# A state-space mixer on one core: the opening of the kernel rearranged, and the later images' statistics in column tiles

## The chip, the cores and the metric

The kernel runs on one NeuronCore of a Trainium2 chip. A NeuronCore has five engines, each with its own queue of instructions that it works off in order: TensorE (PE in the profile; PEld is its loading of weights), VectorE (DVE), ScalarE (ACT), GpSimd (POOL) and SyncE (SP), which here only issues DMAs. They work at the same time and wait for each other through semaphores. Sixteen DMA engines move data between HBM (the large memory) and SBUF (the working memory of 128 partitions); matrix products land in PSUM, eight banks of 512 float32 numbers per partition. The metric is the device time of one execution in microseconds (us).

## The reference

Four images of 128 channels and 96 x 96 pixels are normalised per group of four channels, and each is read as a sequence in four directions (rows, columns, and both reversed). Each sequence goes through the same mixer, and the four results are fused and added to the input:

```python
def _scan1d(x, ...):
    t = _grouped1x1(x, in_proj_w, in_proj_b, G)
    u, gate = (t[:, :HID], t[:, HID:])
    u = jax.nn.silu(u)
    u = lax.conv_general_dilated(u, dw_w, ..., feature_group_count=HID)   # 5 taps
    s = _conv1x1(u, ssm_in_w)
    a = DMIN + (DMAX - DMIN) * jax.nn.sigmoid(_conv1x1(u, ssm_delta_w, ssm_delta_b))
    bb = jnp.tanh(_conv1x1(u, ssm_b_w, ssm_b_b))
    cc = jnp.tanh(_conv1x1(u, ssm_c_w, ssm_c_b))
    prefix = jnp.cumsum(jnp.log(a), axis=-1)
    hst = jnp.exp(prefix) * jnp.cumsum(bb * s * jnp.exp(-prefix), axis=-1)
    u = u + _conv1x1(cc * hst + ssm_d[None, :, None] * s, ssm_out_w)
    u = _grouped1x1(u * jax.nn.sigmoid(gate), mix_w, mix_b, G)
    return _conv1x1(u, out_proj_w, out_proj_b)
...
x = x + conv_ref(_gn(x), ...)      # four directions, then fuse_w, fuse_b
```

All numbers are float32.

## The kernel before

**Units of work.** A sequence is cut into `NS` = 6 stages of 16 lines; every fourth column belongs to one residue p, so a stage has R = 4 residues of N = 384 positions. A *pair* is one residue of one stage in a direction and its reverse: two units. An image has 24 pairs in the order V (columns), then 24 in H (rows): 192 pairs in all. `pair(t)` issues the work of pair t together with that of neighbours: the front of the stage R pairs ahead, the recurrence of earlier pairs, and the output (gate, mixing, accumulation in `acc`) of pair t - LAG = t - 6. The order on each engine is the order in which the program issues it; it is fixed by hand. `start()` issues what stands before pair 0, `tail()` what stands after the last.

**A front.** `in_proj` multiplies the rows `x_in` of a stage with the normalised weights `wn`, in 32x32 tiles of the array, four columns at a time; `silu` (L495 in ACT) takes it out of PSUM to `sil`, with the bias `bnorm`. A burst is the eight tiles of one half j and one residue g. Then `conv` and `conv_less` (PE, from `sil` with the weights `band` and `less`) give half of `u`, which ACT copies out (L632, L634), and `taps` gives the other half: tap 0 on ACT (L649), taps 1 to 4 on VectorE (L651), each waiting for the one before. `proj` multiplies u with `main` and ACT takes tanh of it (`tm`, L683), and with that the pair's recurrence can begin. The fronts of the later half of a sequence use `sil` kept in HBM by `keep_silu` and loaded back.

**Statistics.** `bn_stats` (L282 for image 0, from `acc`, into which x is loaded anyway; L412 for the later images, from chunks `xs` loaded one pair ahead in two buffers) takes 24 pieces of 384 columns per image. `stats_finish` is a generator whose pieces are issued between other work: bn_aggr, the group means by a product with `gmean` (L187), the variance (L199), the inverse deviation, the weights `wn` times it, and the biases by `wn` times the group means (L235 and sixteen 32x32 products in L238), read by VectorE (L239).

**The opening.** SP issues the loads of x (`load_x`, growing pieces) and then step 0's `x_in`; ACT's queue issues the loads of the weights `small`, `fuse` and `main`. At most eight DMAs are under way by the program's eight DMA semaphores: each issue waits for the eighth before it. POOL builds gmean, the identity, band and less. PE and ACT fold the output's weights: `w_of` = out_proj x fuse per direction (L364), `w_fin` = mix x w_of (L371), `b_fin` the bias (L379), before image 0's statistics are through; `stay_busy` (L286) are matmuls without use, 512 or 256 columns wide, put into the gaps. Then `start()`:

```python
        for g in range(R):
            burst(0, g)
        for g in range(R):
            silus(0, g)
        new_u(0)
        for g in range(R):
            burst(1, g)
            silus(1, g)
            after_front(0, g)
            ...
```

`after_front` issues on SP the loads of step 1's rows, one residue of half 1 at a time and half 0 after the last. `proj` of pair 0 has step 1's first front (residue 0) between its two halves.

Of the kernel before, what the change touches and what calls it, by code (L numbers as in the profile page):

```python
# [42 lines left out]
F32 = mybir.dt.float32  # L43
# [4 lines left out]
P = 128  # L48
# [8 lines left out]
R = 4  # L57
# [10 lines left out]
def conv_preact_kernel(  # L68
# [106 lines left out]

    def stats_finish(b):
# [10 lines left out]
        nc.tensor.matmul(pm[:, 0:1], gmean, mv[:, 0:1], start=True, stop=True)  # L187
# [10 lines left out]
        for e in range(2):  # L198
            nc.tensor.matmul(pv[:, e : e + 1], gmeans[:, e, :], ex, start=True, stop=True)  # L199
# [35 lines left out]
        nc.tensor.matmul(pb[:, 0:4], wn, gm4, start=True, stop=True)  # L235
        for g in range(4):
            for q in range(R):
                mm(pb[:, 4 + g : 5 + g], q, wn[0:32, 32 * g : 32 * g + 32], mean[0:32, :], True, True)  # L238
        nc.vector.tensor_sub(bn, b_in, pb[:, 0:8])  # L239
# [33 lines left out]
    def load(src, name, pool=wp):  # L273
        t = pool.tile(list(src.shape), F32, tag=name, name=name)
        nc.scalar.dma_start(t, src)
        return t
# [7 lines left out]
    def stay_busy(n):  # L284
        if n:
            nc.tensor.matmul(  # L286
                bank(free[0] ^ 1)[:, :n], w_fin[:, 0, 0, :],
                w_fin.rearrange("p d j c -> p (d j c)")[:, :n], start=True, stop=True,
                skip_group_check=True,
            )  # L290

# [6 lines left out]
    prep = tc.tile_pool(name="prep", bufs=1)  # L298
    pp = prep.__enter__()
    load_x([(0, 1), (1, 2), (3, 3)])  # L300
    w_small = load(small, "small")
    load_x([(6, 4)])
    w_out_fuse = load(fuse, "fuse", pp)
    load_x([(10, 4)])
    w_main = load(main, "main")
    load_x([(14, 4), (18, 4), (22, 2)])
    for s in range(2):
        load_front(0, s, half(s), slice(0, R))
    for i in range(UB):
# [13 lines left out]
    nc.vector.tensor_scalar_mul(b_proj[64:P, 0:1], b_proj[64:P, 0:1], 0.5)  # L323
    nc.vector.tensor_scalar_mul(
        w_proj[:, :, 2 * MH : 3 * MH], w_proj[:, :, 2 * MH : 3 * MH], 0.5
    )


# [11 lines left out]
    id32 = pp.tile([P, 32], F32, name="id32")  # L340
    ident = pp.tile([P, P], F32, name="ident")
# [18 lines left out]
    w_of = pp.tile([P, 4, 2, P], F32, name="w_of")  # L360
    for d in range(4):
        for j in range(2):
            pt = bank(2 * (d % 4) + j)
            nc.tensor.matmul(  # L364
                pt[:, :P], w_out[:, bass.ts(j, P)], w_fuse[:, d, :], start=True, stop=True
            )
            nc.scalar.copy(w_of[:, d, j, :], pt[:, :P])
    for d in range(4):
        for j in range(2):
            pt = bank(2 * (d % 4) + j)  # L370
            nc.tensor.matmul(  # L371
                pt[:, :P], w_mix[:, j, :], w_of[:, d, j, :], start=True, stop=True
            )
            nc.scalar.mul(w_fin[:, d, j, :], pt[:, :P], 0.5)
    pb = bank(0)
    terms = [(w_of[:, d, j, :], b_mix[:, j : j + 1]) for d in range(4) for j in range(2)]
    terms += [(w_fuse[:, d, :], b_out) for d in range(4)]
    for i, (lhsT, rhs) in enumerate(terms):
        nc.tensor.matmul(  # L379
            pb[:, 0:1], lhsT, rhs, start=(i == 0), stop=(i == len(terms) - 1)  # L380
        )
    nc.scalar.activation(b_fin, pb[:, 0:1], AF.Identity, bias=b_fuse)
    for _ in range(4):
        stay_busy(512)
    prep.__exit__(None, None, None)
# [19 lines left out]
    def load_chunks(t):  # L405
        for b, c in chunks_of(t):
            chunks[b, c] = wk.tile([P, SC], F32, tag="xs", name=f"xs_{b}_{c}")
            nc.sync.dma_start(chunks[b, c], xr[b, :, bass.ts(c, SC)])
# [721 lines left out]
```

## Time and profile before

| | us |
|---|---|
| runs shown | 1824.41, 1825.7, 1827.61 (median 1825.7) |
| the profiled execution | 1830.29 |
| its span, first to last instruction | 1828.6 |
| mean granted clock of TensorE | 0.993 of full |

The page gives busy time, its share of the span, and the number of instructions for each engine; then 40 equal slices of the span, a digit for tenths of a slice that an engine was busy:

```profile
PE   7999999999999999999999999999999999999998
ACT  4888888988888888898888888888888888888974
PEclk7999999999999999999999999999999999999999
```

Only the first slice (45.7 us) and the last are not full. PEclk is the clock granted to TensorE, in tenths. The waits of the first 55 us, by the waiting engine and line, who released it, and the sum, the number and the longest:

```profile
PE psum L364 <- DMA fuse<-in_fuse: 6.5, 1, 6.5
DVE bn L282 <- DMA acc<-in_xr: 3.3, 2, 1.7
PE psum L134 <- DMA x_in<-in_xs: 3.2, 1, 3.2
ACT psum L649 <- DVE u L651: 2.4, 1, 2.4
PE psum L187 <- DVE mv L184: 2.1, 1, 2.1
```

`mm`, the helper of all tiled products, is line 134, so groups of tiled matmuls are told apart by what they read and write: `psum<-x_in,wn` is in_proj, `psum<-sil,band` conv, `psum<-u,main` proj, `psum<-u,w_fin` the output.

### The profile page before, as it was taken

The page shows a single profiled execution, that of the slowest core. Times are in us where ns is not written, and L with a number is a line of the kernel's source. Part 1 is how long each engine was busy: PE and PEld are TensorE (multiplying, and loading weights), DVE is VectorE, ACT ScalarE, POOL GpSimd, SP SyncE. Part 2 cuts the span into 40 slices and gives each one's busy share as a digit, 9 for nine tenths or more (in the row PEclk, how much of TensorE's full clock was granted, in tenths as well). Part 3 has the DMA queues.
Part 4 walks back from the last instruction along what each step waited for, and adds up shares of the span by engine and source line. Part 5 has one row for each costly group of instructions (what it writes and reads, how often), then busy time and mean ns, then how long its engine had stood idle before and what let it go on. Part 6 is the DMA issues. An engine that isn't in the chain of part 4 may idle for free.

```text
span 1828.6 us, 56926 instructions
## 1 busy us (share of the span) xinstructions
PE 1805.3 (99%) x24068; PEld 653.1 (36%) x24068; DVE 1451.0 (79%) x1451; ACT 1566.5 (86%) x2762; POOL 1423.7 (78%) x1469
## 2 busy tenths in 40 slices
PE   7999999999999999999999999999999999999998
PEld 3333333333333333333333333333333333333333
DVE  5788878877788888887788888877877878777886
ACT  4888888988888888898888888888888888888974
POOL 2478887878778888777877888788778788887785
PEclk7999999999999999999999999999999999999999
DMA  5765464543975567244596557543477734535434
GB/s 182 205 199 173 148 189 116 169 156 130 278 260 180 167 180 214 98 147 139 180 306 224 167 169 207 141 142 120 159 230 221 245 126 152 192 106 179 148 122 156
DMA packets 147823, 321.17 MB, mean 176 GB/s; under 512 B 14192, under 2 KB 115696, under 8 KB 147568
## 3 DMA queue, kind: packets, MB, share of 16 engines
q1 hardware_dynamic: 147136, 316.56, 53.8%
q8 instruction: 190, 3.11, 0.7%
q10 hardware_dynamic: 432, 0.96, 0.1%
q14 instruction: 65, 0.53, 0.1%
HBM read 185.21 MB, written 132.25 MB: 174 GB/s over the span
## 4 chain that ended last, share of the span: by engine, by line
PE 96%; ACT 1%; DVE 1%; DMA 1%; issue 0%; SPq 0%; DVEq 0%
PE psum L134 83%; PE psum L520 8%; PE psum L514 5%; DMA acc<-in_xr 0%; DVE bn L282 0%; ACT sil L495 0%; DVE u L600 0%; ACT psum L649 0%; DMA x_in<-in_xs 0%; DVE psum L651 0%; PE psum L286 0%; ACT psum L528 0%; PE psum L199 0%; ACT u L632 0%; ACT t L689 0%
## 5 line engine op out<-in xcount | busy, mean ns | idle before, releaser
L651 DVE SCALAR_TENSOR_TENSOR psum<-sil,small,psum 128x768 f32<-128x768 f32 x576 | 589.1, 1023 | 35.1 <-ACT psum L649 8.3
L134 PE MATMUL psum<-u,w_fin 128*32 128x384 f32 x6176 | 552.3, 487 | 0.2 <-ACT t L689 0.2
L600 DVE SCALAR_TENSOR_TENSOR u<-gate,psum 128x768 f32<-128x768 f32 x376 | 349.8, 953 | 248.4 <-ACT gate L537 110.5
L134 PE MATMUL psum<-u,main 128*32 128x384 f32 x6144 | 536.4, 490 | 0.2
L770 POOL TENSOR_TENSOR acc<-ys,acc 128x384 f32<-128x384 f32 x374 | 410.7, 1119 | 31.2 <-ACT ys L751 9.2
L724 POOL TENSOR_TENSOR t<-t,t 64x384 f32<-64x384 f32 x191 | 232.2, 1216 | 154.6 <-DVE t L718 70.8
L134 PEld LDWEIGHTS psum<-u,w_fin 128*32 128x32 f32 x6176 | 188.8, 110 | 321.7 <-issue 216.5
L134 PEld LDWEIGHTS psum<-u,main 128*32 128x32 f32 x6144 | 182.0, 110 | 328.1 <-issue 198.9
L691 POOL TENSOR_SCALAR t<-tm 64x384 f32<-64x384 f32 x191 | 177.1, 927 | 153.7 <-ACT tm L683 100.1
L528 ACT COPY psum<-u 128x768 f32<-128x768 f32 x352 | 276.7, 799 | 22.0 <-DVE u L651 11.3
L134 PE MATMUL psum<-sil,band 128*32 128x384 f32 x3072 | 287.2, 491 | 0.0
L725 POOL TENSOR_TENSOR t<-t,t 64x384 f32<-64x384 f32 x191 | 246.5, 1291 | 15.0
L520 PE MATMUL psum<-t,main 32*128 32x384 f32 x1536 | 241.4, 513 | 3.3 <-ACT psum L528 2.6
L649 ACT ACTIVATE psum<-sil,small 128x768 f32<-128x768 f32 x192 | 174.1, 907 | 65.4 <-DVE u L600 54.9
L537 ACT ACTIVATE gate<-psum,bnorm 128x384 f32<-128x384 f32 x384 | 192.0, 582 | 30.2 <-PE psum L514 28.6
L692 POOL TENSOR_TENSOR t<-t,tm 64x384 f32<-64x384 f32 x192 | 195.1, 1016 | 15.4 <-ACT t L684 0.2
L651 DVE SCALAR_TENSOR_TENSOR u<-sil,small,psum 128x768 f32<-128x768 f32 x192 | 194.9, 1015 | 7.8
L495 ACT ACTIVATE sil<-psum,bnorm 128x385 f32<-128x385 f32 x384 | 192.3, 583 | 6.4 <-PE psum L134 4.3
L134 PE MATMUL psum<-sil,less 64*32 64x384 f32 x3072 | 168.1, 495 | 0.0
L514 PE MATMUL psum<-x_in,wn 32*128 32x384 f32 x768 | 157.5, 527 | 1.5 <-DVE bnorm L239 1.1
L727 POOL COPY t<-t 64x384 f32<-64x384 f32 x188 | 141.0, 750 | 15.5 <-PE psum L134 3.6
L134 PEld LDWEIGHTS psum<-sil,band 128*32 128x32 f32 x3072 | 90.8, 109 | 171.8 <-issue 95.5
(92 smaller groups left out, 1496.7 us busy)
## 6 DMA issues: line engine op xcount, KB each, us to landing
sil<-sil SPq DMA_DIRECT2D x128, 770.0 KB, 6.6
kept<-gate SPq DMA_DIRECT2D x80, 768.0 KB, 3.7
gate<-kept SPq DMA_DIRECT2D x76, 768.0 KB, 5.1
x_in<-in_xs SPq DMA_DIRECT2D x192, 96.2 KB, 2.5
out<-acc SPq DMA_DIRECT2D x48, 384.0 KB, 8.3
acc<-in_xr SPq DMA_DIRECT2D x38, 384.0 KB, 7.1
xs<-in_xr SPq DMA_DIRECT2D x72, 192.0 KB, 4.9
x_in<-in_xs SPq DMA_DIRECT2D x184, 48.1 KB, 4.0
```

Source lines behind the costliest of these rows:

```text
L134: nc.tensor.matmul(o[r, : rhs.shape[-1]], lhsT, rhs, start=start, stop=stop, skip_group_check=True)
L495: nc.scalar.activation(sils[step][:, s, j, g, :], bank(bk)[:, : N + 1], AF.Silu, bias=bn[:, 1:2] if j else bn[:, 4 + g : 5 + g],)
L514: nc.tensor.matmul(bank(to)[:, :N], stats[un["b"]][0][r, s, :], x_in[s][r, q, off : off + N], start=True, stop=True)
L520: nc.tensor.matmul(bank(SSM + 2 * s + j)[:, :N], w_so[r, bass.ts(j, P)], z[r, :], start=bi not in seeded, stop=True, skip_group_check=True)
L528: nc.scalar.copy(psum[:, SSM + 2 * s : SSM + 2 * s + 2, :N], us[bi][:, s])
L537: nc.scalar.activation(gv[:, s, j, :], bank(to[2 * s + j])[:, :N], AF.Tanh, bias=bn[:, 2 + j : 3 + j], scale=0.5,)
L600: nc.vector.scalar_tensor_tensor(v, g, 1.0, pz, ALU.add, ALU.mult)
L651: nc.vector.scalar_tensor_tensor(us[i][:, :, 1, :] if k == K - 1 else part, src, w_tap[:, k : k + 1], part, ALU.mult, ALU.add,)
L692: nc.gpsimd.tensor_mul(ta[0:64, p, :], tb[0:64, :], tm[0:64, :])
L724: engine.tensor_mul(ta[0:64, p, :], tb[64:P, :], ta[64:P, p, :])
L725: engine.tensor_add(tb[0:64, :], ta[0:64, p, :], tb[0:64, :])
L770: adder.tensor_add(part, y, part)
```

## The change

1. `load_x` takes x first and in smaller first pieces, all on SP; `fuse` and `main` come behind x on SP, and only `small` is issued by ACT. The scalings of `b_proj` and `w_proj` go from VectorE to POOL, behind band and less.
2. The folding of the output's weights moves into `start()`: `outer` (L364 before) between the pieces of the statistics, with one copy per direction on ACT (three) or VectorE (one); `inner` between the bursts, taken out by VectorE two directions at a time. `b_fin` is summed over directions by POOL (four additions) and then needs three matmuls instead of twelve, behind pair 0's conv. `filler`, matmuls on loaded x, replaces `stay_busy`: five of 512 columns and one of 128.
3. `start()` is in a new order, given below; pair 0's first tap is on VectorE; the loads of step 1's rows (`load_rows`) and the keeping of step 0's sil stand in `start()`. In pair 0's `proj` the front of step 1 stands before both halves, with the next pair's first tap in its middle.
4. The chunks `xs` of the later images are loaded two pairs ahead, in four buffers.
5. The products of the statistics are column tiles (`product`: four of 32 columns). For the later images the biases of the 32x32 kind come from one small copy, one product with the mask and four tiles with the identity, one piece later than before. Where a pair accumulates two waiting units, a piece of the statistics stands ahead of conv_less.

```diff
 
+    def product(o, lhsT, rhs):
+        for c in range(4):
+            mm(o, c, lhsT[:, 32 * c : 32 * c + 32], rhs, True, True)
+
...
-        nc.tensor.matmul(pm[:, 0:1], gmean, mv[:, 0:1], start=True, stop=True)
+        product(pm[:, 0:1], gmean, mv[:, 0:1])
...
-        nc.tensor.matmul(pb[:, 0:4], wn, gm4, start=True, stop=True)
-        for g in range(4):
+        product(pb[:, 0:4], wn, gm4)
+        if b == b0:
+            for g in range(4):
+                for q in range(R):
+                    mm(pb[:, 4 + g : 5 + g], q, wn[0:32, 32 * g : 32 * g + 32], mean[0:32, :], True, True)
+            nc.vector.tensor_sub(bn, b_in, pb[:, 0:8])
+        else:
+            nc.vector.tensor_sub(bn[:, 0:4], b_in[:, 0:4], pb[:, 0:4])
+            spread = sp.tile([P, 4], F32, tag="spread", name=f"spread_{b}")
+            shift = sp.tile([P, 1], F32, tag="shift", name=f"shift_{b}")
+            nc.vector.tensor_copy(shift, pb[:, 0:1])
+            nc.vector.tensor_scalar_mul(spread, gmask, shift)
+            yield
+            pq = bank(free[0])
             for q in range(R):
-                mm(pb[:, 4 + g : 5 + g], q, wn[0:32, 32 * g : 32 * g + 32], mean[0:32, :], True, True)
-        nc.vector.tensor_sub(bn, b_in, pb[:, 0:8])
+                mm(pq[:, 0:4], q, id32, spread, True, True)
+            nc.vector.tensor_sub(bn[:, 4:8], b_in[:, 4:8], pq[:, 0:4])
...
-    load_x([(0, 1), (1, 2), (3, 3)])
-    w_small = load(small, "small")
-    load_x([(6, 4)])
-    w_out_fuse = load(fuse, "fuse", pp)
-    load_x([(10, 4)])
+    w_small = load(small, "small", nc.scalar)
+    load_x([(0, 1), (1, 1), (2, 1), (3, 2), (5, 2), (7, 3), (10, 4), (14, 4), (18, 4), (22, 2)])
+    w_out_fuse = load(fuse, "fuse")
     w_main = load(main, "main")
-    load_x([(14, 4), (18, 4), (22, 2)])
...
+    nc.gpsimd.tensor_scalar_mul(b_proj[64:P, 0:1], b_proj[64:P, 0:1], 0.5)
+    nc.gpsimd.tensor_scalar_mul(
+        w_proj[:, :, 2 * MH : 3 * MH], w_proj[:, :, 2 * MH : 3 * MH], 0.5
+    )
...
-            chunks[b, c] = wk.tile([P, SC], F32, tag="xs", name=f"xs_{b}_{c}")
+            chunks[b, c] = wk.tile([P, SC], F32, tag="xs", bufs=4, name=f"xs_{b}_{c}")
...
-            if k == 0:
+            if k == 0 and first:
+                first.tensor_scalar_mul(part, src, w_tap[:, 0:1])
+            elif k == 0:
                 nc.scalar.activation(part, src, AF.Copy, scale=w_tap[:, 0:1])
...
-            if i == 0 and (e, j) == (0, 1):
-                front(R, (5, 4, 2, 3))
+            if i == 0 and (e, j) == (0, 0):
+                first = front_parts(R, (5, 4, 2, 3), half=True)
+                next(first)
+                next(first)
+                first_tap(2)
+                for _ in first:
+                    pass
...
             accumulate(waiting.pop(0), w[1], *final)()
             free[0] = w[0]
+            stats_piece()
             if not between:
                 conv_less(i, banks)
-            stats_piece()
         if old:
...
-        if t + 1 < NU // 2:
-            load_chunks(t + 1)
+        if t + 2 < NU // 2:
+            load_chunks(t + 2)
...
-        keep_silu((1, 2, 1, 0)[t] if t < R else 0)
...
+        w_of = wp.tile([P, 4, 2, P], F32, name="w_of")
+        def filler(n):
+            nc.tensor.matmul(
+                bank(7)[:, :n], accf[:, bass.ds(10 * SC, P)], accf[:, bass.ds(10 * SC, n)],
+                start=True, stop=True,
+            )
+        def outer(d, i, copy):
+            for j in range(2):
+                nc.tensor.matmul(
+                    bank(i)[:, bass.ts(j, P)], w_out[:, bass.ts(j, P)], w_fuse[:, d, :],
+                    start=True, stop=True,
+                )
+            copy(w_of[:, d].rearrange("p j c -> p (j c)"), bank(i)[:, : 2 * P])
+        def inner(ds, i):
+            for n, (d, j) in enumerate((d, j) for d in ds for j in range(2)):
+                nc.tensor.matmul(
+                    bank(i)[:, bass.ts(n, P)], w_mix[:, j, :], w_of[:, d, j, :],
+                    start=True, stop=True,
+                )
+            to = w_fin[:, ds[0] : ds[-1] + 1].rearrange("p d j c -> p (d j c)")
+            nc.vector.tensor_scalar_mul(to, bank(i), 0.5)
         pieces = stats_finish(b0)
-        for wait in (0, 256, 512, 0, 0):
-            next(pieces, None)
-            stay_busy(wait)
+        for n in (512, 512, 512):
+            filler(n)
+        next(pieces)
+        for n in (512, 512):
+            filler(n)
+        next(pieces)
+        outer(0, 0, nc.scalar.copy)
+        outer(1, 1, nc.scalar.copy)
+        next(pieces)
+        outer(2, 4, nc.scalar.copy)
+        next(pieces)
+        outer(3, 5, nc.vector.tensor_copy)
+        filler(128)
+        for _ in pieces:
+            pass
         sils[0] = wk.tile([P, 2, 2, 4, N + 1], F32, tag="sil", name="sil_0")
-        banks = ((2, 3), (4, 5), (6, 7), (0, 1)), ((2, 3), (4, 5), (2, 3), (4, 5))
+        banks = ((2, 3), (6, 7), (0, 1), (4, 5)), ((2, 3), (6, 7), (4, 5), (2, 3))
         def burst(j, g):
             for s in range(2):
...
                 silu(0, g, s, j, banks[j][g][s])
             edges(0, g, j, nc.vector)
+        def load_rows(j, r):
+            for s in range(2):
+                load_front(1, s, slice(64 * s + 32 * j, 64 * s + 32 * j + 32), r)
         for g in range(R):
             burst(0, g)
-        for g in range(R):
-            silus(0, g)
+        silus(0, 0)
+        burst(1, 0)
+        silus(0, 1)
+        burst(1, 1)
+        silus(0, 2)
+        inner((0, 1), 0)
+        inner((2, 3), 1)
+        for w in (w_of, w_fuse):
+            for e in (2, 1):
+                nc.gpsimd.tensor_add(w[:, 0:e], w[:, 0:e], w[:, e : 2 * e])
+        load_rows(0, slice(0, R))
+        load_rows(1, slice(0, 1))
+        silus(0, 3)
         new_u(0)
-        for g in range(R):
-            burst(1, g)
-            silus(1, g)
-            after_front(0, g)
-            if g < 2:
-                taps(0, (g,))
-            if g == 1:
-                conv(0, head_banks(0))
-                conv_less(0, head_banks(0))
-        taps(0, (2, 3, 4))
+        burst(1, 2)
+        silus(1, 0)
+        taps(0, (0,), nc.vector)
+        burst(1, 3)
+        load_rows(1, slice(1, R))
+        silus(1, 1)
+        taps(0, (1,))
+        conv(0, head_banks(0))
+        silus(1, 2)
+        taps(0, (2,))
+        silus(1, 3)
+        conv_less(0, head_banks(0))
+        taps(0, (3, 4))
+        to_keep.extend((0, g) for g in range(R))
+        keep_silu(R)
+        pf = bank(3)
+        terms = [(w_of[:, 0, j, :], b_mix[:, j : j + 1]) for j in range(2)] + [(w_fuse[:, 0, :], b_out)]
+        for i, (lhsT, rhs) in enumerate(terms):
+            nc.tensor.matmul(pf[:, 0:1], lhsT, rhs, start=(i == 0), stop=(i == len(terms) - 1))
+        nc.scalar.activation(b_fin, pf[:, 0:1], AF.Identity, bias=b_fuse)
```

## The prediction

> **What bounds the kernel now.** I read the page's busy shares first, then the wait table of TensorE (PE) over the whole span, then the opening: the timeline, the chain of waits, and busy time cut at the steps of the granted clock.
>
> ```profile
> PE 1805.3 (99%) x24068; PEld 653.1 (36%) x24068; DVE 1451.0 (79%) x1451; ACT 1566.5 (86%) x2762; POOL 1423.7 (78%) x1469
> ```
>
> PE has work all the time. In 100 to 1700 us its waits come to 1.1 us (gate matmuls behind the bias tile bnorm of the next image). So nothing that leaves PE's work alone is worth more than a few us there. Time can only come from the opening, or from shorter PE work. The chain of waits of the opening, by start, length and holder:
>
> ```profile
> 2.20 8.54 DMA acc<-in_xr
> 10.74 0.02 issue
> 10.76 8.52 DVE bn L282 x18
> 19.28 0.02 issue
> 19.30 0.81 DVE mv L184
> ...
> 37.83 3.31 DMA x_in<-in_xs
> 41.13 0.14 issue
> 41.27 8.01 PE psum L134 x80
> ```
>
> Until 10.74 us the bound is the arrival of x, then VectorE's 18 statistics at 8.52 / 18 = 0.473 us each, then the scalar chain, then at 37.83 the first projection of step 1, which waits for its input rows. The third view is busy time in stretches; the figure after the POOL count is the clock, then DMA share and GB/s:
>
> ```profile
> 13.62:17.03 3.41, 3.41 (x16) 2.12 (x16) 3.41 (x9) 0.26 (x1) 0.00 (x0) 1.00 1.03 379
> 17.03:20.44 3.41, 1.35 (x5) 0.41 (x3) 3.04 (x6) 0.00 (x0) 0.00 (x0) 1.00 1.08 207
> 20.44:23.85 3.41, 3.41 (x10) 2.20 (x10) 1.49 (x8) 1.15 (x2) 0.00 (x0) 0.50 0.81 202
> 23.85:27.25 3.40, 3.40 (x67) 1.64 (x73) 0.38 (x3) 1.22 (x4) 0.00 (x0) 0.50 0.02 5
> 27.25:30.66 3.41, 3.41 (x65) 1.65 (x56) 0.31 (x6) 2.78 (x6) 0.00 (x0) 0.50 0.00 0
> 30.66:34.06 3.40, 3.40 (x31) 0.59 (x16) 0.18 (x3) 3.24 (x7) 0.00 (x0) 0.50 0.22 48
> 37.47:40.89 3.42, 0.64 (x8) 0.00 (x0) 2.76 (x3) 1.04 (x3) 0.00 (x0) 1.00 0.62 156
> 40.89:44.30 3.41, 3.04 (x40) 0.83 (x44) 2.83 (x3) 1.95 (x5) 0.00 (x0) 0.50 0.09 18
> ```
>
> The clock steps at 20.44, 34.06, 40.89 and 47.71: multiples of 3.41 us. It is half for 20.4 us in all, behind two gaps (18.2 to 20.25 and 38.1 to 41.27). While the 32x32 in_proj tiles alone run (23.85 to 30.66) PE counts as fully busy and the clock stays half: busy is not enough, the array must be filled.
>
> **What the Trainium skill says.** "TensorE: Matmul & The Clock Gate", Part 1, describes an activity monitor that samples in free-running windows of about 3.4 us and halves the clock of an idle array; the steps agree (13.62 and 6.82 us apart). It says that sustained activity releases the clock; here one busy window (20.44) did not, so I require a well-filled one. "DMA: Bandwidth & Descriptors", Issuing engines are not separate DMA queues: transfers of different issuers interleave on the same engines. The trace agrees: fuse (0.52 MB) landed at 6.5 although x had been issued first. "TensorEngine Tiling (Array Packing)", Key Properties: a change of tiling mode drains the array. The trace shows 0.62 us without a weight load ahead of each change of tile form, the full-array statistics products among them, though PE itself shows no idle there.
>
> **Part 1: x first.** The DMA moved 0.25 MB by 3 us, 0.93 by 5, and then 0.42 MB per us. Before, 0.96 MB of weights shared this with 4.72 MB of x: 10 chunks of x and all weights (2.93 MB) had moved at 9.7 us and the data was usable at 10.7, so landing is bytes plus 1.0 us. Now only small (0.04) is beside x. Chunks to 17 (3.58 MB) land at 12.25, 18 to 21 (4.37) at 14.1, the last two at 15.1. VectorE is as fast as the DMA (one chunk of 0.197 MB per 0.473 us), so it trails by the last large group: 14.2 + 6 x 0.473 = 17.0, against 19.28. **Minus 2.3 us.** VectorE's two weight scalings go to POOL, idle from 10.9 to 45.8. Bound: 15.4 if no chunk is waited for, 18 if the small first pieces start slowly. The bytes ahead of step 0's x_in are the same as before, so its two loads land near 21 as before (issue 8.9 and 9.6, 11.5 us); fuse lands near 16.3 and main 17.25, before their users at 18 and 20.5.
>
> **Part 2: the scalar chain.** From 19.30 to the first silu at 26.57 took 7.3 us, of it 0.56 us in which wn was ready (23.60) and PE was still in a filler (to 24.16), and cold matmuls. Now: five fillers of 512 columns start when chunks 10 to 13 have landed (10.4). One takes 0.86 warm (14.51 to 18.2 holds four), about 1.75 cold; with the clock up after one full window they end between 15.8 and 17.5. mv 17.8; mean 18.45; ex 19.07; two outer products (four matmuls of 0.25 warm) sit in that gap; pv 19.3; var 19.85; std 20.05; wn 20.5 to 20.96; outer 2, 3 and a short filler end by 20.85; pb and 16 small ones 0.6 us to 21.6; bias 22.15; silu at **22.2** (ACT's table load, 1.28, and one copy end there too). **Minus 4.35 in all.** x_in at 21 leaves 0.6 us of slack.
>
> **Part 3: fronts of step 0.** Before, ACT's silus came in pairs at 26.57, 27.80, 29.09 and 30.37: 1.28 us apart, PE's cold price of a burst of 8 tiles; ACT's own price is 1.06. Warm, I take half, 0.64. inner (8 matmuls, 128 wide, 1.8 warm, 3.5 cold) now stands on PE before bursts (1,2) and (1,3).
> *Warm throughout:* 16 silus x 0.53 from 22.2 end at 30.7, taps at 32.7, first tm 35.0, second 41.
> *Middle:* 3.8 us of bursts alone (21.6 to 25.3) hold most of a clock window, so I take one drop at about 23.9, as between 23.85 and 30.66 now. Two bursts and inner run cold (inner 26.7 to 30.2), inner fills a window and lifts the clock near 30.7. Silus (1,2) and (1,3) end at 33.1, conv and less (1.47 and 0.88) at 34.25, the copy to u at 35.2, taps at 35.2 (40.36 before).
> *Cold:* a window that holds the gap before mv drops the clock at about 19.5; silu at 23, inner 30 to 33.5, first tm 42.5.
>
> **Part 4: step 1.** Its rows are now issued as soon as their readers are done, and not behind step 0's last burst: the j = 0 rows behind the fourth burst at 24.2, landing by 29, so the wait of 3.15 us at 41.27 goes. What is late next is u. In the middle case: in_proj of step 1 34.9 to 36.2 (it waits for b_fin to read bank 3), proj to 39.1, first tm 39.2 (before 45.09), conv and less to 41.4, in_proj 42.4, proj, second tm at 45.2 (before 52.84, of which some 2 us were the second cold stretch). **Minus 7.6 us.** From here PE and ACT (3.9 of 4 us busy in 52 to 60) run the same pairs.
>
> **Part 5: queues.** SP carries all. Four stores of sil (0.79 MB each, 3.15 MB) move from 44 to 72 us to about 33 to 44, ahead of the xs chunks and step 2's rows. At the 214 to 319 GB/s that such stretches moved, they end by 44 to 47, with the first xs needed at 47.4. Now xs holds VectorE at 63.0 by 2.15 us and PE then by 0.94; loading two pairs ahead should remove most: **minus 0.5** (range 0 to 0.9). Later images' xs waits hold no PE.
>
> **Part 6: statistics in column tiles.** Per image now: pm 0.31, pv 0.54, pb and the 16 means 0.75, wait 0.36: 1.96 us. After: 4, 8, 4 and 4 matmuls in the mode of their neighbours, which I put at 0.1, 0.2, 0.1, 0.1 from 16 small ones in 0.43, and two waits for VectorE of 0.5 each (three and two small VectorE steps of 0.16; what is queued behind are the gate matmuls, and ACT's tanh behind those). 1.5 us, x3 images: **minus 1.3**. Bound: minus 3 without waits, plus 3 if each wait grows to 1.2.
>
> **Sum.** 7.6 + 0.5 + 1.3 = 9.4 us. The profiled execution (1830.3 with what lies round its span of 1828.6) would be 1820.9. It is 4.6 above the median of the runs; taking the difference over, 1825.7 - 9.4 = **1816.3 us**.
>
> **Rivals.** *Warm throughout* (0.20): second tm at 41, 11.8 + 1.8: 1812. For: PE is filled from 10.4 on. Against: tile bursts alone did not hold or lift the clock. *The array is not kept warm* (0.24): the fillers have no wait among them, so all five run at once and end before mv, leaving 0.3 to 2.1 us idle; about 4.3 + 1.3 from parts 1 and 4: 1820. *No difference* (0.08): parts 1 and 4 are taken back by step 0's x_in at 23 or later and by xs in pairs 2 and 3: 1825. *Slower* (0.05): the four stores. If they drain below 150 GB/s, xs lands after 56.8 and VectorE, then the taps, then PE stand by more than the 9.4 won; at 120 GB/s the 3.54 MB are through at 62.5, 15 us late: 1831. Against: the same stores now land in 5.4 to 8.9 us each with others in flight.
>
> **Numbers.** The middle case has 0.43, its own range 1814 to 1819. A difference of 0.2% (3.7 us) is what a measurement can tell from none. The cold case holds some outcomes near that line: faster 0.85, same 0.09, slower 0.06. For 8 in 10 the range covers warm and cold and the bounds of part 6: 1810.5 to 1822.
>
> **What would show it.** Last bn near 17; fillers in one row from 10.4 with a gap before pm; first silu near 22.2 (with x_in as its releaser I was wrong on slack); clock half for one or two windows between 20 and 31; in_proj of step 1 with no DMA wait; second tm near 45; from 100 us the same rows, with two short waits of gate matmuls per image. A first silu after 25, or an xs wait over 3 us near 47, would make me wrong.

## The result

| | before | changed |
|---|---|---|
| median, first comparison (11 runs each) | 1828.6 us | 1822.32 us |
| lowest and highest | 1824.41, 1832.63 | 1819.54, 1828.29 |
| median beside the experiments (before, 99 runs); of all comparisons (changed, 26 runs) | 1827.8 | 1821.9 |
| the profiled execution | 1830.29 | 1821.96 |
| its span | 1828.6 | 1820.2 |

The ratio of the means is 0.9974, with a 95% interval from 0.9961 to 0.9987: 4.8 us less (2.4 to 7.1), where 9.4 had been forecast. Two later comparisons gave 0.9967 (0.9952 to 0.9983) and 0.9956 (0.9944 to 0.9968), that is 6.0 and 8.0 us. From one profiled execution to the other the time fell by 8.3 us, more than the ratios of the first two comparisons give. How far a difference of two profiles can be trusted is the subject of this study.

The busy shares of the changed kernel, first line of the page:

```profile
PE 1792.3 (98%) x24074; PEld 645.5 (35%) x24074; DVE 1454.6 (80%) x1462; ACT 1562.5 (86%) x2748; POOL 1428.2 (78%) x1475
```

PE's busy time fell by 13 us with six instructions more: the same matmuls, fewer of them at half clock. The chain of waits in the opening (start, length, holder):

```profile
3.62 8.53 DMA acc<-in_xr
12.15 0.03 issue
12.17 6.66 DVE bn L298 x14
18.84 0.02 issue
18.86 0.82 DVE mv L188
...
36.10 0.05 issue
36.15 12.76 DMA xs<-in_xr
48.91 0.02 issue
48.94 1.06 DVE bn L387 x2
```

The statistics of image 0 end only 0.44 us earlier than before (mv at 18.86 against 19.30). The wait for step 1's rows at 37.83 is gone, and in its place stands the first chunk `xs` of the next image, which took 12.76 us to land. Busy time in the stretches that the prediction used (PE, PEld, DVE, ACT and POOL; then the clock, the DMA share and GB/s):

```profile
13.62:17.03 3.41, 3.41 (x6) 1.30 (x5) 3.41 (x9) 0.00 (x0) 0.00 (x0) 1.00 1.02 409
17.03:20.44 3.41, 2.41 (x17) 1.12 (x16) 2.90 (x7) 0.00 (x0) 0.00 (x0) 1.00 1.07 253
20.44:23.85 3.41, 3.41 (x81) 2.50 (x79) 1.94 (x10) 2.69 (x6) 0.39 (x1) 1.00 1.01 222
23.85:27.26 3.41, 3.32 (x92) 1.99 (x88) 0.29 (x5) 2.94 (x7) 0.00 (x0) 1.00 0.24 64
37.49:40.90 3.41, 3.41 (x72) 1.02 (x64) 3.30 (x4) 2.69 (x7) 1.96 (x2) 1.00 1.07 265
40.90:44.30 3.40, 2.97 (x47) 1.44 (x40) 2.33 (x3) 3.03 (x7) 0.00 (x0) 1.00 1.07 189
```

The stretches are not the clock's own windows in this execution: its first recorded step, up, is at 16.37, and the next, down, at 1798.13. So between the statistics and the tail no window is at half clock, where before 20.4 us of the opening were. I call a window at half clock lost, and what runs in it cold. To see where the time went I follow the start of each pair's `tm` (the tanh behind its proj) in four profiled executions. "Before, again" is the unchanged kernel in a further execution (the first of experiment 1), "changed, again" the changed one in the last of experiment 7:

| tm of pair | before | before, again | changed | changed, again |
|---|---|---|---|---|
| 0 | 45.09 | 39.10 | 37.97 | 38.17 |
| 1 | 52.84 | 45.02 | 44.13 | 44.32 |
| 6 | 86.95 | 79.05 | 78.05 | 78.12 |
| 24 | 251.82 | 243.92 | 242.92 | 242.99 |
| 30 | 309.43 | 301.53 | 300.11 | 300.30 |
| 186 | 1750.22 | 1742.25 | 1740.12 | 1740.29 |
| 191 (last) | 1792.72 | 1784.74 | 1782.61 | 1782.77 |
| end of the span | 1828.6 | 1822.1 | 1820.2 | 1818.8 |

Read down the columns. The changed kernel is 8.9 us ahead of the first column at pair 6 and stays there to pair 24; it gains 0.42, 0.41 and 0.38 at the three later images' statistics; and it gives 1.8 back behind the last pair. But the unchanged kernel itself, in another execution, is already 7.9 us ahead of its own first profile at pair 6, and 8.0 at pair 186. Most of the opening's 8.9 us is a difference between two executions of one kernel. (Two more profiles of the kernel before, with a gap filled in each, are 5.6 and 6.2 us ahead of the first at pair 6; a third one of the changed kernel, in experiment 1, is at 36.74 at pair 0 and at 77.76 at pair 6, so that of 1.2 us at the start 0.3 are left.) The windows of "before, again", cut at the steps of its own clock:

```profile
14.64:18.05 3.41, 3.41 (x8) 1.86 (x8) 3.41 (x9) 0.26 (x1) 0.00 (x0) 0.50 1.04 308
18.05:21.46 3.41, 3.17 (x12) 1.57 (x11) 2.31 (x7) 0.00 (x0) 0.00 (x0) 1.00 1.08 225
21.46:24.87 3.41, 3.37 (x79) 2.24 (x86) 1.14 (x6) 2.28 (x5) 0.00 (x0) 1.00 0.45 113
31.69:35.10 3.41, 1.79 (x24) 0.42 (x16) 2.85 (x4) 2.05 (x5) 0.00 (x0) 1.00 0.47 113
35.10:38.51 3.41, 2.19 (x44) 0.77 (x48) 2.34 (x3) 2.18 (x4) 0.00 (x0) 1.00 0.28 75
```

The windows lie 1.0 us later against the program than in the first profile, and one of them, at 14.64, is lost. PE's four `stay_busy` matmuls happen to fall into it, run cold up to 18.05 (they last from 15.11 to 20.24 instead of 14.51 to 18.2), and so fill the gap ahead of `mv` that dropped the clock in the first profile. The wait for step 1's rows is still there, 2.8 us before 36.33, but a boundary at 35.10 cuts it in two: each window keeps PE busy for 1.79 and 2.19 of 3.41 us, and the clock stays up. In the first profile nearly the whole wait lay in one window (0.64 us busy) and cost the next two their clock.

### The profile page after: what moved, and what is told of

Same layout as the page of the kernel before. It is cut to its first block, busy times and chain, and to the rows that moved or that the text cites. A ratio compares the mean times of both kernels' runs of the same rounds, so it can differ in the third digit from the quotient of the medians.

```text
span 1820.2 us, 56934 instructions
## 1 busy us (share of the span) xinstructions
PE 1792.3 (98%) x24074; PEld 645.5 (35%) x24074; DVE 1454.6 (80%) x1462; ACT 1562.5 (86%) x2748; POOL 1428.2 (78%) x1475
## 4 chain that ended last, share of the span: by engine, by line
PE 94%; ACT 2%; DVE 2%; DMA 1%; issue 0%; SPq 0%; POOL 0%; DVEq 0%; ACTq 0%; POOLq 0%
PE psum L134 81%; PE psum L497 8%; PE psum L491 5%; DMA xs<-in_xr 1%; ACT psum L505 1%; ACT sil L470 1%; DVE psum L630 1%; DMA acc<-in_xr 0%; DVE bn L298 0%; ACT u L611 0%; DVE u L577 0%; DVE u L630 0%; ACT psum L628 0%; DVE t L702 0%; SPq L296 0%
```

## The experiments

"Before beside" is the unchanged kernel on the same chip, in the runs of the same comparison.

**1. Both kernels again, a filled gap, no fillers.** Unchanged:

> The kernel before, unchanged, to see the granted clock of every execution beside its time. Clock theory (the single profiled executions differ from the other runs because each execution meets the free-running clock windows at another phase): executions spread over some 8 us, and those with a lower mean clock are the longer ones, about 1.8 us for each 0.001 of mean clock (3.65 us at half speed, half of it lost); the mean clock lies at 0.992 to 0.996. Rival (the spread has nothing to do with the clock, or the profile of before was no different from other runs): no order between clock and time, all clocks alike.

> The changed kernel, unchanged, on the same chip. Clock theory: mean clock 0.994 to 0.999, above that of before, same slope of about 1.8 us for 0.001, best executions near 1819.5 and worst near 1828; at equal clock the changed kernel is still 3 to 6 us faster than before (order of the work, earlier rows of step 1, statistics). Rival (all of the gain is clock): at equal clock the two kernels take the same time.

Then two `stay_busy` matmuls more in the kernel before, and the changed kernel without any filler:

```diff
-    for _ in range(4):
+    for _ in range(6):
         stay_busy(512)
```

> The kernel before with six matmuls of 512 columns without use, not four, ahead of the wait for the first image's statistics, so that PE is busy until the statistics are through. Clock theory: no drop at 20.4 us in the profile, the in_proj bursts run warm, ScalarE's silus follow at 0.53 us each from the first one, the taps of pair 0 end 2 to 4 us earlier, mean clock of the executions up by 0.002 to 0.004, time down by 2 to 4 us. Rival (bursts of 32x32 tiles cannot hold the clock, as the prediction had it): the clock drops one window later, near 24, and the time is within 1 us of before.

```diff
-        for n in (512, 512, 512):
-            filler(n)
         next(pieces)
-        for n in (512, 512):
-            filler(n)
         next(pieces)
...
-        filler(128)
```

> The changed kernel without its six filler matmuls (they write nothing that is read). Clock theory: the opening runs at half clock from the first product to the inner products at least, the first tm is 3 to 5 us later than 37.97, mean clock 0.992 to 0.996, time up by 3 to 5 us and close to before minus 3 to 5. Rival (the fillers do nothing): time and clock as the changed kernel, within 1 us.

| | median | ratio to before beside |
|---|---|---|
| before, again | 1828.01 | 1.0002 (0.9988 to 1.0016) |
| changed, again | 1821.61 | 0.9967 (0.9952 to 0.9983) |
| before, gap filled | 1827.14 | 1.000 (0.999 to 1.0011) |
| changed, no fillers | 1826.67 | 0.9989 (0.9978 to 0.9999) |

The mean clock ordered the executions: by a straight line through the runs of this comparison, 0.001 of it went with 1.5 us in the kernel before and 1.6 in the changed one, where 1.8 was expected. The other expectation was missed. At the same mean clock the changed kernel was to be 3 to 6 us faster; over all comparisons it is 1.0 us faster at 0.998 (1821.36 in 16 runs for 1822.33 in 3) and 1.2 at 0.996 (1825.61 in 5 for 1826.78 in 28). That is nearer to the rival, that all of the gain is clock: the average clock rose from 0.9949 (99 runs) to 0.9973 (26), which at 1.5 us for 0.001 would be some 3.7 of the 5.7 us between the averages of these runs. This is an estimate; the printed clock has steps of 0.001 and misses cold time at the start (see the last section).

Filling the gap ahead of the product with `mv` took away the drop there (the clock stayed up through 20.4) but the drop behind the wait for x_in came, at 37.5, and the average didn't move (the mean clock was 0.9963 for 0.9952). A single hole filled is not worth what it cost in one profile. The fillers are worth more than anything else that was taken out of the change: without them the mean rises by 3.7 us and the median by 5.1. The 22 executions fall into two groups, eight at 1822.0 to 1824.3 and fourteen at 1825.9 to 1828.8; what parts them was not traced. PE in the opening without fillers (start, length, instructions):

```profile
19.27 0.29 PE L134 MATMUL psum<-mv,gmean 128*32 128x1 f32 x8 [19.27 <-DVE mv L188]
19.49 2.07 PE L999 MATMUL psum<-fuse 128*128 128x128 f32 x8
24.46 6.98 PE L134 MATMUL psum<-x_in,wn 32*32 32x385 f32 x96
31.38 3.78 PE L1007 MATMUL psum<-w_of,fuse 128*128 128x128 f32 x16
```

and of the changed kernel with them:

```profile
12.19 6.62 PE L992 MATMUL psum<-acc 128*128 128x512 f32 x10 [12.19 <-DMA acc<-in_xr]
19.81 0.24 PE L134 MATMUL psum<-mv,gmean 128*32 128x1 f32 x8 [1.00 <-DVE mv L188]
19.98 1.16 PE L999 MATMUL psum<-fuse 128*128 128x128 f32 x8
23.07 4.58 PE L134 MATMUL psum<-x_in,wn 32*32 32x385 f32 x96
27.58 2.05 PE L1007 MATMUL psum<-w_of,fuse 128*128 128x128 f32 x16
```

The same 96 records of in_proj take 6.98 us cold and 4.58 warm; pair 0's tm is at 43.64 instead of 37.97.

**2. Fillers that follow the statistics.** The warm-up matmuls wait for every second chunk's statistics up to the mean, so that no gap is left whenever x lands:

```diff
+        for _ in range(6):
+            keep_warm(accf[:, 0:SC])
+        for c in range(9, NSC, 2):
+            keep_warm(stats[b0][:, c, 0:1])
+            keep_warm(accf[:, 0:SC])
```

> The changed kernel with its five warm-up matmuls (three of 512 columns from about 11-12 us, two behind w_out's last quarter) replaced by short ones that wait for every second chunk's statistics until the mean is there: the array is kept in use from about 10 us to the first matmul of the mean, whenever x lands. Theory A (the opening is a draw of free-running clock windows; fillers only decide how often a window is lost): the array is warm at the first call and tm of pair 0 and pair 6 lie within 1 us of the changed kernel's own (37-38 and 77.8-78.1); the median within 1.5 us of the changed kernel's 1821.6. Theory B (the changed kernel still loses opening time in many executions because its fillers end before the mean is there): median 2 to 4 us below it. Theory C (short fillers with holes between them do not raise the clock): first calls cold, pair 6 later by 4-6 us, median about 1825.

Median 1821.59 (0.9966, 0.995 to 0.9983), pair 0 at 38.19 and pair 6 at 78.68, both within 1 us of the changed kernel's: theory A. In this version the mean's product follows the last warm-up matmul without a gap (20.14). The gap of 0.4 to 1.0 us that the changed kernel has there in its three profiles costs nothing that these runs show.

**3. The tail.** PE in the tail of the changed kernel:

```profile
1793.44 1.49 PE L497 MATMUL psum<-t,main 32*128 32x384 f32 x8
1796.95 2.79 PE L497 MATMUL psum<-t,main 32*128 32x384 f32 x8 [2.02 <-ACT psum L505]
```

The same hole of 2.02 us is in the kernel before (L520 behind ACT L528). Two matmuls without use were put into it, in each kernel:

```diff
+            if n == first + 2:
+                for _ in range(2):
+                    nc.tensor.matmul(bank(6), w_fin[:, 0, 0, :], w_fin[:, 0:2].rearrange(...), ...)
             ssm_out(n + 1)
```

> The changed kernel with two matmuls of 512 columns into an unused bank put into the gap of 2.02 us that TensorE has in the tail (1794.9-1797.0, PE L497 waits for ACT L505). Theory A (that gap is what drops the clock for the two windows at 1798-1804.8): the drop at 1798 goes, the time from the last pair's tm to the end falls by 2 to 4 us, median 1818 to 1820. Theory B (what follows is bound by ScalarE and the stores, not by the clock, or the window drops for the gaps after it): the tail within 0.7 us of the changed kernel's, median 1821 to 1823.

> The kernel BEFORE with the same two matmuls in its tail's gap. Theory A (the gap in the tail and its lost windows belong to both kernels; which windows fall is a draw): the median falls by 1.5 to 4 us, to 1823.5-1826, and the drop at 1799-1812 goes in the profiled execution. Theory B (only the changed kernel has this loss in the tail, as a cost of the change): the median stays within 1 us of 1827.1.

First the changed kernel's stretch behind the hole, then that of the version with the hole filled:

```profile
1798.00:1801.40 3.40, 3.40 (x17) 1.10 (x20) 1.91 (x2) 1.85 (x4) 3.25 (x3) 0.52 0.00 0
1801.40:1804.80 3.40, 3.40 (x24) 0.79 (x16) 0.00 (x0) 0.82 (x2) 2.10 (x3) 0.50 0.44 168
```

```profile
1798.00:1801.40 3.40, 3.40 (x37) 1.12 (x36) 1.82 (x2) 2.25 (x4) 3.25 (x4) 1.00 0.00 0
1801.40:1804.80 3.40, 3.40 (x44) 1.25 (x40) 2.29 (x3) 1.63 (x4) 1.94 (x3) 1.00 0.47 183
```

In the same time 37 and 44 matmuls run instead of 17 and 24. From the last pair's tm to the end of the span:

| | us |
|---|---|
| before; again | 35.9; 37.3 |
| changed, three executions | 37.6; 37.5; 36.0 |
| changed, hole filled | 34.4 |
| before, hole filled | 34.2 |

So the 1.8 us that the changed kernel gave back in its tail is no cost of the change: both kernels lose one or two windows there, by the phase, which is where the windows' boundaries fall. All 13 profiles that have this hole show it. In five the hole lay whole in one window, and two windows were lost. In eight a boundary cut it, and still one was lost (in one of the eight, where the cut was 0.06 us from its end, two). The changed kernel's last profile has its hole from 1795.09 to 1797.11 and a boundary at 1796.00; the third line is the lost window:

```profile
1792.59:1796.00 3.41, 2.50 (x24) 0.73 (x12) 2.69 (x4) 0.37 (x1) 2.23 (x3) 1.00 0.08 32
1796.00:1799.41 3.41, 2.31 (x12) 1.04 (x16) 2.37 (x5) 2.01 (x3) 3.18 (x4) 1.00 0.02 5
1799.41:1802.83 3.42, 3.42 (x28) 1.24 (x24) 0.90 (x2) 2.53 (x4) 3.34 (x4) 0.50 0.00 0
```

The medians: changed 1819.23 (0.9957, 0.9939 to 0.9976), before 1825.2 against 1829.66 beside (0.9983, 0.9971 to 0.9995). Five of the seven timed executions of the former had a mean clock of 1.000 and took 1819.0 in the mean; two had 0.997 and took 1824.15. Where those two lost their windows was not traced.

**4. Statistics in full-array products again.** `product` issues one full-array matmul, and the biases of the 32x32 kind come from sixteen small products as before.

> The changed kernel with the statistics' products of the later images as they were before (full-array matmuls, no column tiles); everything of the opening stays. Theory A (the step of 0.4 us per image in the tm starts is the column tiles): the offset of tm against the kernel before stays flat behind pair 6 (change under 0.15 us from pair 24 to 30, 72 to 78, and 126), where the changed kernel has -0.42, -0.39, -0.38 there. Theory B (the steps come from the order of start() or from the clock): they stay at -0.3 to -0.5 each.

The offset of tm against the first profile of before changes by +0.13 from pair 24 to 30, +0.08 from 72 to 78 and +0.12 from 120 to 126, where the changed kernel has -0.42, -0.41 and -0.38. Theory A: the column tiles and the split bias are the gain, 0.5 us per image against this version. The two were put back together, so their shares are not known.

**5. The stores of sil back in `pair()`.**

```diff
+        keep_silu((1, 2, 1, 0)[t] if t < R else 0)
...
-        keep_silu(R)
```

> The changed kernel with the stores of silu(z) issued again in pair's steps (1, 2, 1, 0 of them) instead of all ahead of step 1's rows and behind them. Theory A (the wait of 2.4 us that VectorE still has for the xs chunk at 48.9 is the chunk queued among those stores): the xs chunk is issued at about the same time but lands 3 to 6 us earlier, VectorE's wait there is under 0.5 us, tm_2 to tm_3 takes 5.7 to 6.2 us instead of 6.96, and pair 6 is 0.7 to 1.1 us earlier relative to pair 0. Theory B (xs is late because it is issued late or shares bandwidth with the weights): the wait stays at 1.5-2.5 us and tm_2 to tm_3 at 6.6-7.1.

VectorE's timeline around the first chunk xs, changed kernel and then this version:

```profile
45.54 1.01 DVE L630 SCALAR_TENSOR_TENSOR u<-sil,small,psum 128x768 f32<-128x768 f32 x1
48.94 1.06 DVE L387 BATCH_NORM_STATS2 bn<-xs 128x6 f32<-128x384 f32 x2 [2.38 <-DMA xs<-in_xr]
```

```profile
45.59 1.01 DVE L630 SCALAR_TENSOR_TENSOR u<-sil,small,psum 128x768 f32<-128x768 f32 x1
46.52 1.01 DVE L387 BATCH_NORM_STATS2 bn<-xs 128x6 f32<-128x384 f32 x2
```

No wait is left. In the changed kernel the four stores, issued from 32.02 to 34.73, landed at 37.33, 41.27, 46.25 and 48.31, and the chunk, issued at 36.15, landed behind them at 48.91; in this version it is issued at 32.04, ahead of all stores, and lands at 35.34 (it was expected to be issued at about the same time). Now tm of pair 2 to pair 3 takes 5.87 us instead of 6.96, and pair 6 is 39.42 behind pair 0 instead of 40.08. The one timed execution took 1819.66. By these two profiles moving the stores ahead of the chunks was a loss of 0.7 to 1.1 us within the change (experiment 7 has one in which less of it came back). In the version of experiment 4 the same wait was 3.7 us, and the clock dropped at 55.1; a wait of this kind is a hazard for the clock as well.

**6. Where x comes from.** Three versions of the loads: x in the pieces of before; x issued by SP and ACT in turn; the weights beside x on ACT's queue again.

```diff
-    load_x([(0, 1), (1, 1), (2, 1), (3, 2), (5, 2), (7, 3), (10, 4), (14, 4), (18, 4), (22, 2)])
+    load_x([(0, 1), (1, 2), (3, 3), (6, 4), (10, 4), (14, 4), (18, 4), (22, 2)])
```

> The changed kernel with the pieces of the first image as the kernel before has them (1, 2, 3, 4, 4, 4, 4, 2 chunks) instead of ten with small ones ahead; one queue, weights behind. Theory A (the low rate of 80-260 GB/s at 3.5-5 us, and so the late end of the statistics, comes from the small pieces): the rate there is over 330, bn ends at about 17.0 as forecast, VectorE's waits for x are 3 to 5 us. Theory B (one issuing queue can't keep the engines filled, whatever the pieces): the rate dips as before and bn ends at 17.6 to 18.8.

```diff
-        for c, n in chunks:
-            nc.sync.dma_start(accf[...], xr[...])
+        for i, (c, n) in enumerate(chunks):
+            (nc.scalar if i % 2 else nc.sync).dma_start(accf[...], xr[...])
```

> The changed kernel with its ten pieces of x issued by SP and ScalarE in turn. Theory A (small pieces): the dip stays, bn ends at 17.6 to 18.8. Theory B (one queue's issue rate is the limit): the dip at 3.5-5 us goes to over 330 GB/s and bn ends at about 17.0; first silu about 22.2.

```diff
     w_small = load(small, "small", nc.scalar)
+    w_out_fuse = load(fuse, "fuse", nc.scalar)
+    w_main = load(main, "main", nc.scalar)
     load_x([...])
-    w_out_fuse = load(fuse, "fuse")
-    w_main = load(main, "main")
```

> The changed kernel with the output's weights loaded on ScalarE's queue beside x again (all that x first took away), x's ten pieces on SP as they are. Theory A (the weights beside x cost the statistics 2.3 us, as forecast): mv starts 2 us or more later than the changed kernel's 17.7 to 19.1, that is at 20 or later. Theory B (x's first pieces wait for their own latency, and VectorE, with 0.47 us a chunk, is the bound from 9 us on): mv starts within 1 us, at 18.3 to 19.6, and x first was worth about 0.6 us.

| | start of mv | tm of pair 0 | its one time |
|---|---|---|---|
| before, 4 profiles | 18.92 to 19.30, mean 19.07 | | |
| changed order of loads, 9 profiles | 17.72 to 19.06, mean 18.48 | | |
| x in the pieces of before | 17.90 | 37.34 | 1820.28 |
| x from two queues | 20.51 | 40.35 | 1824.04 |
| weights beside x | 19.12 | 37.45 | 1819.78 |

(The 9 profiles are those of all versions with the changed kernel's loads of x and weights; the 4 those of the unchanged kernel, its filled gap and its filled tail.) With the weights beside x again the statistics end 0.6 us behind the mean of the changed kernel's, as theory B has it, and the kernel is as early at pair 0. It is one execution, though, and 19.12 is nearly within the range of the nine; even the ranges of the nine and the four overlap. VectorE with the weights beside x (idle before, in brackets):

```profile
3.60 0.56 DVE L298 BATCH_NORM_STATS2 bn<-acc 128x6 f32<-128x384 f32 x1 [3.60 <-DMA acc<-in_xr]
5.12 0.56 DVE L298 BATCH_NORM_STATS2 bn<-acc 128x6 f32<-128x384 f32 x1 [0.95 <-DMA acc<-in_xr]
6.75 0.56 DVE L298 BATCH_NORM_STATS2 bn<-acc 128x6 f32<-128x384 f32 x1 [1.08 <-DMA acc<-in_xr]
```

and in the changed kernel itself:

```profile
3.63 1.12 DVE L298 BATCH_NORM_STATS2 bn<-acc 128x6 f32<-128x384 f32 x2 [3.63 <-DMA acc<-in_xr]
5.85 0.56 DVE L298 BATCH_NORM_STATS2 bn<-acc 128x6 f32<-128x384 f32 x1 [1.10 <-DMA acc<-in_xr]
7.89 1.97 DVE L298 BATCH_NORM_STATS2 bn<-acc 128x6 f32<-128x384 f32 x4 [1.48 <-DMA acc<-in_xr]
```

VectorE waits for early pieces either way: 3.4 us in all behind its first statistics in the changed kernel's first profile (2.4 to 3.6 in the nine), 3.8 with the weights beside x, 3.2 to 3.4 in the four profiles of before. With x first these waits are not gone, and that is why 2.3 us were not gained. With small pieces from one queue the DMA's rate fell to 83 and 151 GB/s in the two halves of 4.0 to 5.0 us of the first profile; with the pieces of before it was 310 and 323 there, and still mv came at 17.90, not at 17.0 (and at 19.10 in the last version below, which has these pieces too, with 255 and 258 GB/s). The rate there does not set the end of the statistics: the changed kernel's second profile had 126 and 249 GB/s in these two halves of a microsecond, and its mv came at 17.72, the earliest of all. Two queues made it worse, in one execution: neither theory had that, and the cause stays open. Its first silu came at 27.14, with a lost window from 21.9 to 25.3.

**7. The best version.** Tail filled and stores back in `pair()`; then with the x pieces of before as well; and the changed kernel beside the latter.

> Both improvements at once: the two matmuls in the tail's gap and the stores of silu(z) in pair's steps again. If the two gains are independent (2.4 us for the tail on the median, about 1 us for the wait for xs): median 1817 to 1818.5, ratio to the kernel before 0.994 to 0.995; the array at full clock at 1797-1805, tm_2 to tm_3 5.8 to 6.3 us. If the wait for xs only makes room for another wait, the median is the tail version's 1819.2 or more.

> All that was found to help: the two matmuls in the tail's gap, the stores of silu(z) in pair's steps, x's pieces as the kernel before has them. Theory A (the larger pieces bring the statistics' end forward by 0.5 to 1 us, and all of it reaches the end): median 1817.3 to 1818.0 against 1818.4 without the pieces. Theory B (the opening's start is not seen through the draw of the clock's windows and the DMA's variation): 1818.0 to 1819.2, no difference.

> The changed kernel once more, as it is, on the chip of these runs: 1821 to 1823 (1821.6 and 1822.3 in the runs so far); tm of pair 0 at 36.7 to 38.2, since no window of its opening is lost; the wait for xs of 2.4 us and the drop at 1797-1798 there again.

The first took 1818.39 (0.9947, 0.9927 to 0.9967 against before; 1817.7 to 1819.91 in six executions), the second 1819.0 (0.9949, 0.9934 to 0.9964), the changed kernel beside it 1820.63. By the medians the fixes are worth 1.6 us (second version, same chip) to 3.5 us (first version, against the 26 runs of other chips) beyond the change, though the intervals of the ratios overlap; the pieces of x make no difference that can be seen. In the second version's profile the wait for xs is gone too, but PE waits 0.76 us at 60.35 for step 2's rows, and pair 6 is 40.34 behind pair 0, not 39.4: part of what the stores gave back was taken again by another wait.

## Why the prediction was wrong

**The step that failed is the last one of the sum:** "It is 4.6 above the median of the runs; taking the difference over, 1825.7 - 9.4". The 9.4 us had been read from one execution, and much of it was what that execution lost by its windows: the second profile of the same kernel had 7.9 of the 8.9 us already, and of 99 executions of the kernel before the 39 with a mean clock of 0.992 to 0.994, where the profile (0.993) belongs, took 1827.8 to 1833.1 in the mean of their groups, the 60 with 0.995 to 0.998 took 1822.3 to 1827.8. Most executions had less to lose, so a median was not to be expected to fall by 9.4. The runs show 4.8 us in its place (6.3 between the medians), with 8.3 between the first two profiles.

From 1816.3 to the measured 1822.3 are 6.0 us. Of these 1.0 is that the profiles differ by less than 9.4, 0.4 that the changed kernel's median lies above its own profile, and 4.6 the distance of the profile of before from the median that was used. This last has two parts: the profile was 1.7 above the median of all eleven runs, 1828.6, and the median of the three runs shown, 1825.7, was 2.9 below it. The second part is the chance of three runs and has nothing to do with the change.

The sum to there, 1820.9 for a profiled execution, came close: the three of the changed kernel took 1821.96, 1821.39 and 1820.53. That is in part luck, since its terms were off both ways: 8.7 us at the second tm for 7.6, nothing for 0.5 at the chunks, 1.2 for 1.3 at the statistics, and 1.8 given back in the tail, which the sum did not have.

What the change is worth on the average: 4.8, 6.0 and 8.0 us by the ratios of three comparisons. Of these about 1.2 are the statistics, by the trace; 3.7 to 5.1 go when the fillers go; and at the same mean clock about 1 us is left. So the average gain is mostly windows that are no longer lost. That the rest of the new order brings little beyond these is what is left over, not a measurement of its own.

By the steps:

- **Part 1** was mis-sized: minus 2.3 forecast for x first, 0.6 in the mean of the profiles (19.07 to 18.48), the same when the weights alone are put back, and then nothing of it is seen at pair 0. The waits for the first pieces stay (3.4 us in all, as before); the bound "18 if the small first pieces start slowly" was the right end.
- **Part 2**: first silu at 23.96 for 22.2. The fillers began at 12.19, not 10.4, since chunks 10 to 13 landed later; from mv on the chain took 5.1 us where 4.4 had been counted.
- **Part 3**: the likeliest case was wrong in the mechanism. The tiles of in_proj alone ran from 23.07 to 27.65, longer than a window, and the clock stayed up. A gap of 1.00 us ahead of the mean did not drop it either, so the rival in which the array is not kept warm fell too. The window from 23.20 to 26.61 lies within these tiles. It was the warm case, but its second tm came at 44.13 rather than 41: its silus began 1.8 us later than that case had them, and the first tap stood on VectorE behind the second copy of w_fin (29.67 to 30.36), which waits for `inner`, and began at 30.66 though its input was there at 29.27.
- **Part 4** was right that in_proj of step 1 has no DMA wait. The second tm, at 44.13 for 45.2, is near by luck: the forecast had two lost windows that did not come, and earlier silus than came.
- **Part 5** was not gained: the chunk xs behind the stores landed at 48.9, not by 47, and the wait for it is 2.4 us for the 2.15 of before. From tm of pair 2 to pair 6 the changed kernel takes 28.1 to 29.1 us in three profiles, the kernel before 28.4 to 29.0 in four. The slower rival named this mechanism; by experiment 5 its price was about 1 us, not 15.
- **Part 6** was right: minus 1.2 for minus 1.3.
- **Not in the forecast**: the tail, whose windows fall by the phase, plus 1.8 here.

"TensorE: Matmul & The Clock Gate", Part 1, says in the Trainium skill that the window is free-running and that the number of cold matmuls therefore varies between runs of one kernel. I had used the period from it and not this consequence; the runs agree with it, with 7.9 us between two executions of the unchanged kernel.

## What to carry to other kernels

A profile is one draw. Where the time to be won stands at half clock, ask first what of it another execution of the same kernel would lose (the mean clock beside each run tells), and where the change removes the lost stretches, do not subtract the profile's whole difference from a median; a median of three runs can itself be off (here by 2.9 us). What a hole of about 2 us on PE costs depends on where the window boundaries fall: the tail's hole cost two windows when it lay whole in one and one when it was cut, while two holes of the opening that were cut, of 2.4 and 2.8 us, cost none. So look for such holes at both ends of the kernel, and don't expect one filled hole to show in the average (experiment 1: nothing; the tail of before: 3.1 us by the ratio). And stores that are moved earlier stand ahead of every later load on their queue.

## What the runs showed of the hardware

- The busy share of a window alone does not tell whether the clock is lost behind it. In the openings windows of 3.41 us with 1.35 us of PE work and less lost it, and windows with 1.51 us (the filled tail's profile of before, 16.00 to 19.41), 1.77 and more kept it. In the tails windows lost it with 1.4 to 1.5 us, and also with 1.8 to 2.3 (2.31 in the lines of experiment 3).
- Every drop but one, and but those at the very end of the span, had a hole of 2.0 us or more on PE in the window before it or across its start. The one: in the second profile of before the clock dropped at 14.64 without a hole, behind 2.2 us of matmuls of one column (from 12.45).
- 32x32 tiles alone hold a raised clock over a whole window (23.20 to 26.61 in the changed kernel) though they did not raise a lowered one in before (24.94 to 30.66). So "the array must be filled", as the prediction read the latter, is not what keeps the clock.
- The clock column reads 1.00 ahead of the first recorded step even where matmuls are cold: without fillers the clock printed for the profiled execution is 0.999, while two of the `outer` products took 2.07 us for 1.16 and the first recorded step, up, is at 36.15. The mean clock misses cold time at the start.
- 0.001 of the mean clock went with 1.2 to 1.7 us of the time in both kernels (least squares over the runs of each comparison), and the spread of 9 us in the changed kernel and 12.5 in before is mostly that (r squared 0.74 to 0.95, where the clock varied at all).
